# A new order for the opening of an adaptive-layernorm block, with separate buffers for two modulation rows

## Chip, cores and metric

The kernel runs on one core of a Trainium2 chip. The metric is the device time of one execution in microseconds, as the median of repeated runs.

## The reference, cut to what matters

The program computes one transformer-like block on x of shape (2, 4096, 512). A conditioning vector c gives six modulation rows per batch entry. The first half of the block normalizes x, applies two of the rows, computes three projections with a linear recurrence along the sequence, and adds the result to x through a third row. The second half does the same with a feed-forward part in blockwise FP4.

```python
mod = (_silu(L0_c) @ L0_wmod).reshape(L0_c.shape[0], 6, 1, -1)
sa, ca, ga, sb, cb, gb = (mod[:, 0], mod[:, 1], mod[:, 2], mod[:, 3], mod[:, 4], mod[:, 5])
ga = (2 * (ga >= 0) - 1) * jnp.maximum(jnp.abs(ga), 0.25)      # gb likewise
h = _layernorm(x, axis=-1) * (1 + ca) + sa
x = x + ga * attn(h, W_qkva, gamma)
h = _layernorm(x, axis=-1) * (1 + cb) + sb
x = x + gb * ffn(h, w_gate, w_up, w_down)
# attn: hn = h / |h| * sqrt(512) * gamma;  q, kv, a = split(hn @ W_qkva.T)
#       y_t = sigmoid(a_t) * y_{t-1} + kv_t;  result q * y
```

## The kernel before, in words

**Stages.** The program has two halves. The first (the loop over slots from line 751 on) does the recurrence: x is cut into 16 blocks of 512 rows, and each block into four output groups e of 128 channels, so that there are 64 slots. In a slot, `mix` (line 382) multiplies the transposed block `xT` with the transposed weights `wqT` of group e: three parts (2, 1, 0: gate, kv, q), each with 12 matmuls of 128x512, in fp16 high and low halves. In slot 0 alone, the matmuls are cut into four pieces of 128 columns, one for each row tile. The second half (from line 939 on) is the feed-forward part.

**What has to be ready before the first matmuls of slot 0.** `start()` (line 640) does it, in one order written out by hand. Inside `tc.manual_schedule` (line 747), the instructions of every engine run in the order in which the program issues them; SP, which issues the loads and the transposes, also runs in that order. `start()` mixes these chains:

- Modulation. `load_mod(s, pieces)` (208) loads the 512x512 weights of row s; `mod_spread` (216) multiplies them on TensorE with the conditioning vector `sc` spread over 128 columns, which gives the row on all partitions; ACT copies the two results to `ca[0]` and `sa[0]`. `mod_rows` (228) makes the same row for both batch entries in two partitions, and `mod_store` (255) copies that to `row` on ACT and writes it to DRAM by a DMA of POOL. `row` has one buffer. The PSUM tiles of these steps (`side`, 75) have two buffers.
- Weights of group e and part p. `load_part` (205), multiply by gamma (`gamma_qkva`, 278, on POOL or DVE), sum of squares on ACT (`square_qkva`, 281), inverse root (`inverse_qkva`, 285: one DVE step and a power on POOL), high half (`hi_qkva`, 301, on ACT or DVE), low half on DVE and the transpose on SP's DMA queue (`lo_qkva`, 310). `gain_qkva` (293) prepares the scale for the outputs.
- Rows of x, tile g of 128 rows. `norm_load` (328), `norm_moments` (336, DVE), `norm_stats` (339, DVE and POOL), `norm_center` (342, DVE), `norm_shift` (345, DVE), `norm_square` (348, ACT), `norm_gain` (355, DVE or POOL, then a power on POOL), `norm_hi` (362, ACT), `norm_lo` (368, DVE, then the transpose on SP's queue into `xT`).

**What start leaves to the slots.** Weights of groups 0 and 1 and the tiles 0 to 3 are finished in `start()`; tile 4 is carried up to its gain. Slot 0 issues, in this order: the matmuls of e=0, `mod_columns(2)` on TensorE, `norm_hi(4)`, the gammas (POOL) and squares (ACT) of group 2, `norm_moments(6)`, `norm_lo(4)`, and the steps of tile 5 up to its gain, then `scale_qkva(2)`. Slot 1 begins with e=1's matmuls and the halves and transposes of group 2, and goes on with tile 5 and the gammas of group 3; slot 2 has the transposes of group 3, slot 3 the last tile of block 1. `gates`, `scan`, `read_out` and `halves` treat the outputs of the slot before; `halves` (423) writes `yh`, one buffer, from slot 1 on.

Of the kernel before, what the change touches and what calls it, by code (L numbers as in the profile page):

```python
# [7 lines left out]
F32 = mybir.dt.float32  # L8
# [3 lines left out]
AF = mybir.ActivationFunctionType  # L12
# [5 lines left out]
P = 128  # L18
D = 512
KC = D // P  # L20
B = 2
# [22 lines left out]
def tile_adaln_block(  # L44
# [13 lines left out]
    V, A, G, T, S = nc.vector, nc.scalar, nc.gpsimd, nc.tensor, nc.sync  # L58
# [19 lines left out]
    mhalf = ctile([P, 4], F32, "mhalf")  # L78
# [103 lines left out]
    apool = pa.enter_context(tc.tile_pool(name="apool", bufs=1))  # L182

    def atile(shape, dtype, name, bufs=1):
        return apool.tile(shape, dtype, name=name, tag=name, bufs=bufs)
# [13 lines left out]
    with nc.allow_non_contiguous_dma(reason="c is 4 KB"):  # L199
        for b in range(B):  # L200
            S.dma_start(cT[:, :, b], c[b].rearrange("(k p) -> p k", p=P))
    A.activation(sc, cT, AF.Sigmoid)
    V.tensor_mul(sc, sc, cT)

    def load_part(e, part):
        S.dma_start(wq[e, part], w_qkva[part * D + e * P : part * D + (e + 1) * P, :])

    def load_mod(s, pieces=1):
        w = KC // pieces
        for k in range(0, KC, w):  # L210
            S.dma_start(
                wm[s][:, k : k + w, :],
                wmod[k * P : (k + w) * P, s * D : (s + 1) * D].rearrange("(k p) e -> p k e", p=P),
            )
# [13 lines left out]
    def mod_rows(s):  # L228
        pm = side((P, D))
        for k in range(KC):  # L230
            T.matmul(pm[:B, :], sc[:, k, :], wm[s][:, k, :], start=k == 0, stop=k == KC - 1)
        return s, pm[:B, :]
# [19 lines left out]
            out=dst, in0=dst, scalar=1.0, in1=mag, op0=ALU.subtract, op1=ALU.mult  # L252
        )

    def mod_store(s, pm):
        row = apool.tile([B, D], F32, name="row", tag="row", bufs=1)
        if s == 5:
            signed_floor(row, pm, apool.tile([B, D], F32, name="mag", tag="y", bufs=3))
        else:
            A.activation(row, pm, AF.Copy, bias=1.0 if s in (1, 4) else 0.0)  # L260
        G.dma_start(modd[s], row)
# [12 lines left out]
    def load_qkva(e):  # L274
        for part in (2, 1, 0):
            load_part(e, part)

    def gamma_qkva(e, part, engine=G):
        engine.tensor_tensor(wq[e, part], wq[e, part], gam, ALU.mult)

    def square_qkva(e, part):
        sq = work.tile([P, D], BF16, name="sq", tag="sq", bufs=1)
        A.activation(sq, wq[e, part], AF.Square, accum_out=us[:, e, part : part + 1])

    def inverse_qkva(e, a=0, b=3):
        V.tensor_scalar(rs[:, e, a:b], us[:, e, a:b], 1e-36, 2.0**-28, ALU.max, ALU.mult)
        G.tensor_tensor(rs[:, e, a:b], rs[:, e, a:b], mhalf[:, : b - a], ALU.pow)
# [5 lines left out]
    def gain_qkva(e):  # L293
        V.tensor_scalar(
            us[:, e, :], us[:, e, :], 1e-36, 2.0**-28 / (XGAIN * XGAIN), ALU.max, ALU.mult
        )
        G.tensor_tensor(us[:, e, :], us[:, e, :], phalf[:, :3], ALU.pow)
# [3 lines left out]
    def hi_qkva(e, part, on_act):  # L301
        w = wq[e, part]
        hl = whl[e, part] = new_hl()
        rsc = rs[:, e, part : part + 1]
        if on_act:
            A.activation(hl[:, 0, :], w, AF.Copy, scale=rsc)
        else:
            V.tensor_scalar(hl[:, 0, :], w, rsc, None, ALU.mult)

    def lo_qkva(e, part):  # L310
        w = wq[e, part]
        hl = whl.pop((e, part))
        r = part * KC + e
        V.scalar_tensor_tensor(
            out=hl[:, 1, :],
            in0=w,
            scalar=rs[:, e, part : part + 1],
            in1=hl[:, 0, :],
            op0=ALU.mult,
            op1=ALU.subtract,  # L320
        )
        S.dma_start_transpose(wqT[:, :, r * P : (r + 1) * P], flat(hl))
# [5 lines left out]
    def norm_load(g):  # L328
        i, t = divmod(g, KC)
        if i not in xrows:  # L330
            xrows[i] = apool.tile([P, KC, D], F32, name="xr", tag="xr", bufs=4)
        xld[g] = xrows[i][:, t, :]
        b, t0 = divmod(g * P, N)
        S.dma_start(xld[g], x[b, t0 : t0 + P, :])

    def norm_moments(g):
        xstat[g] = moments(xld[g])

    def norm_stats(g):
        xstat[g] = mean_rstd(xstat[g])  # L340

    def norm_center(g):
        xh[g] = center(xld.pop(g), xstat[g][0], ca[g * P // N])

    def norm_shift(g):
        shift(xh[g], xstat.pop(g)[1], sa[g * P // N])

    def norm_square(g):
        h = xh[g]
        sq = work.tile([P, D], BF16, name="sq", tag="sq", bufs=1)  # L350
        ss = small.tile([P, 1], F32, name="ss", tag="ss")
        A.activation(sq, h, AF.Square, accum_out=ss)
        xh[g] = h, ss

    def norm_gain(g, engine=V):
        h, ss = xh[g]
        engine.tensor_scalar(ss, ss, 1e-24, 1.0 / (D * XGAIN * XGAIN), ALU.max, ALU.mult)
        rn = small.tile([P, 1], F32, name="rn", tag="rn")
        G.tensor_tensor(rn, ss, mhalf[:, 0:1], ALU.pow)
        xh[g] = h, rn  # L360

    def norm_hi(g):
        h, rn = xh[g]
        hl = new_hl()
        A.activation(hl[:, 0, :], h, AF.Copy, scale=rn)
        xh[g] = h, rn, hl

    def norm_lo(g, xT):
        h, rn, hl = xh.pop(g)
        V.scalar_tensor_tensor(  # L370
            out=hl[:, 1, :], in0=h, scalar=rn, in1=hl[:, 0, :], op0=ALU.mult, op1=ALU.subtract
        )
        t = g % KC
        S.dma_start_transpose(xT[:, :, t * P : (t + 1) * P], flat(hl))
# [263 lines left out]
    sa = [ctile([P, D], F32, "sa0", tag="mod_s0"), None]  # L638

    def start():  # L640
        load_mod(1, 2)
        norm_load(0)
        load_mod(0, 2)
        load_part(0, 2)
        S.dma_start(gam, gamma.partition_broadcast(P))
        norm_load(1)
        load_part(0, 0)
        norm_load(2)
        load_part(0, 1)
        load_part(1, 2)  # L650
        load_part(1, 0)
        load_part(1, 1)
        norm_load(3)
        norm_load(KC)
        norm_load(KC + 1)
        pc = mod_spread(1, 0)
        ps = mod_spread(0, 0)
        r1 = mod_rows(1)
        r0 = mod_rows(0)
        norm_moments(0)  # L660
        norm_stats(0)
        A.activation(ca[0], pc, AF.Copy, bias=1.0)
        norm_center(0)
        gamma_qkva(0, 2, G)
        norm_moments(1)
        norm_stats(1)
        square_qkva(0, 2)
        gamma_qkva(0, 0, V)
        inverse_qkva(0, 2, 3)
        norm_moments(2)  # L670
        square_qkva(0, 0)
        gamma_qkva(0, 1, V)
        hi_qkva(0, 2, True)
        inverse_qkva(0, 0, 1)
        square_qkva(0, 1)
        lo_qkva(0, 2)
        hi_qkva(0, 0, True)
        inverse_qkva(0, 1, 2)
        norm_stats(2)
        norm_center(2)  # L680
        hi_qkva(0, 1, True)
        lo_qkva(0, 0)
        lo_qkva(0, 1)
        load_mod(2)
        gamma_qkva(1, 2, G)
        A.copy(sa[0], ps)
        norm_center(1)
        norm_shift(0)
        square_qkva(1, 2)
        norm_shift(1)  # L690
        norm_square(0)
        norm_square(1)
        norm_gain(0)
        norm_moments(3)
        norm_gain(1)
        norm_shift(2)
        norm_hi(0)
        norm_hi(1)
        norm_lo(0, xT)
        norm_square(2)  # L700
        norm_lo(1, xT)
        norm_gain(2)
        norm_stats(3)
        norm_center(3)
        norm_hi(2)
        norm_shift(3)
        norm_lo(2, xT)
        norm_square(3)
        norm_gain(3)
        gamma_qkva(1, 1, V)  # L710
        gamma_qkva(1, 0, V)
        norm_hi(3)
        inverse_qkva(1, 2, 3)
        square_qkva(1, 1)
        norm_lo(3, xT)
        square_qkva(1, 0)
        inverse_qkva(1, 1, 2)
        hi_qkva(1, 2, False)
        inverse_qkva(1, 0, 1)
        lo_qkva(1, 2)  # L720
        hi_qkva(1, 1, True)
        hi_qkva(1, 0, True)
        lo_qkva(1, 1)
        lo_qkva(1, 0)
        gain_qkva(0)
        load_qkva(2)
        norm_moments(KC)
        norm_stats(KC)
        norm_center(KC)
        norm_load(KC + 2)  # L730
        load_qkva(3)
        norm_shift(KC)
        norm_square(KC)
        norm_moments(KC + 1)
        norm_gain(KC)
        norm_stats(KC + 1)
        gain_qkva(1)
        mod_store(*r1)
        mod_store(*r0)

    units, coming = [], []
    gate = rows = None
# [278 lines left out]
```

## Time and profile before

| | us |
|---|---|
| median of 3 runs | 1957.3 (1956.27 to 1957.99) |
| the profiled execution | 1956.05 |
| its span, first to last instruction | 1954.2 |
| PE busy in the span | 1909.9 |
| DVE, ACT, POOL busy | 1607.7, 991.3, 423.8 |
| PE busy from 0 to 93 us | 62.7 of 93 |

PE is TensorE's matmul queue, DVE VectorE, ACT ScalarE, POOL GpSimd, SP the engine that issues most DMAs. Times in the lines are microseconds from the span's start. A line of the view in order of time gives start, length, engine, source line, instruction, output and inputs with their shapes, and in brackets how long the engine had been idle and what released it. A line that stands for several instructions (x36) is one stretch of the same kind. The mean granted TensorE clock of the execution is 0.992 of full speed.

### The profile page before, as it was taken

To read this page: it belongs to the slowest core of one execution; us is meant where nothing else is said; L and a number is where in the kernel's file an instruction comes from. 1 tells how busy PE (TensorE), PEld (TensorE's weight loads), DVE (VectorE), ACT (ScalarE), POOL (GpSimd) and SP (SyncE) were. 2 spreads that over 40 slices of the span, in tenths; PEclk is the share of its full clock that TensorE was granted. 3 is DMA by queue.
4 is the path that set the end of the run, shared out by engine and by line. 5 is a ranking of instruction groups with operands and counts; after the bars stand their busy time and mean duration, and the time that the engine had idled before them with its cause. 6 is when DMAs were issued, how large, how long until landed. Compare 5 with 4: busy or idle time off the path is not lost.

```text
span 1954.2 us, 25678 instructions
## 1 busy us (share of the span) xinstructions
PE 1909.9 (98%) x9220; PEld 902.4 (46%) x9220; DVE 1607.7 (82%) x2673; ACT 991.3 (51%) x1704; POOL 423.8 (22%) x603
## 2 busy tenths in 40 slices
PE   6699999999999999999999999999999999999998
PEld 4244444444444444444444444444444444444444
DVE  5777879999958988888888888888888888888865
ACT  3444467777755544544444454444445444444432
POOL 3554456666530100000000000001000000000000
PEclk8899999999999999999999999999999999999999
DMA  7597679999853343443343335334433433433333
GB/s 232 106 250 205 172 156 207 205 205 199 180 126 63 72 89 62 74 82 63 62 82 74 62 74 91 64 63 87 74 63 73 82 64 62 81 75 63 67 62 51
DMA packets 482943, 206.39 MB, mean 106 GB/s; under 512 B 439494, under 2 KB 440774, under 8 KB 482816
## 3 DMA queue, kind: packets, MB, share of 16 engines
q1 hardware_dynamic: 468080, 170.98, 40.9%
q0 software_dynamic: 14736, 33.78, 10.2%
q8 instruction: 72, 1.18, 0.3%
q14 instruction: 55, 0.45, 0.1%
HBM read 62.85 MB, written 33.58 MB: 49 GB/s over the span
## 4 chain that ended last, share of the span: by engine, by line
PE 79%; issue 5%; DVE 1%; DMA 1%; ACT 0%; POOL 0%; SPq 0%; POOLq 0%; ACTq 0%; DVEq 0%
PE mm L856 44%; PE sd L903 21%; PE mm L391 14%; DMA ld<-out_dram 0%; POOL out_dram L926 0%; DMA xT<-hl 0%; DVE ld L172 0%; DVE y L418 0%; DVE hl L370 0%; DVE ld L166 0%; DVE st L153 0%; DVE y L409 0%; ACT sq L583 0%; DVE xn L106 0%; SPq L265 0%
## 5 line engine op out<-in xcount | busy, mean ns | idle before, releaser
L856 PEld LDWEIGHTS <-x2T 128*128 128x128 f16 x4608 | 450.9, 98 | 469.4 <-issue 1.2
L391 PE MATMUL mm<-xT,wqT 128*128 128x512 f16 (+1 forms) x2412 | 510.2, 375 | 26.9 <-DMA wqT<-hl 13.1
L856 PE MATMUL mm<-wuT,x2T 128*128 128x512 f16 (+1 forms) x2304 | 487.7, 361 | 1.0 <-DVE hid L876 1.0
L856 PE MATMUL mm<-wgT,x2T 128*128 128x512 f16 (+1 forms) x2304 | 487.7, 361 | 0.0
L903 PE MATMUL sd<-wdT,hT 128*128 128x512 f16 x2112 | 465.8, 379 | 0.0
L391 PEld LDWEIGHTS <-wqT 128*128 128x128 f16 x2412 | 233.7, 100 | 305.0 <-issue 28.9
L903 PEld LDWEIGHTS <-hT 128*128 128x128 f16 x2112 | 206.7, 98 | 242.7
L871 ACT ACTIVATE silu<-mm,u 128x512 f32<-128x512 f32 (+1 forms) x192 | 124.7, 650 | 286.1 <-PE mm L856 282.4
L876 DVE SCALAR_TENSOR_TENSOR hid<-mm,u,silu 128x512 f32<-128x512 f32 (+1 forms) x192 | 128.6, 673 | 139.6 <-PE mm L856 130.6
L585 POOL TENSOR_SCALAR rstd<-vs 128x1 f32<-128x1 f32 x64 | 14.6, 228 | 985.9 <-ACT sq L583 985.9
L143 ACT ACTIVATE u<-ud,rms 128x1 f32<-128x1 f32 x64 | 18.9, 295 | 278.0 <-DVE rms L139 278.0
L120 ACT ACTIVATE sle<-sl 128x512 f16<-128x512 f32 (+2 forms) x162 | 146.9, 907 | 0.0
L113 ACT ACTIVATE she<-sh 128x1408 bf16<-128x1408 bf16 (+1 forms) x128 | 128.3, 1003 | 4.0
L926 POOL DMA_DIRECT2D out_dram<-o x65 | 58.0, 897 | 276.2 <-DVE o L923 272.3
L409 DVE TENSOR_TENSOR_SCAN y<-sig,cy,mm 128x512 f32<-128x512 f32 x56 | 71.7, 1280 | 49.3 <-ACT sig L403 22.1
L122 DVE SCALAR_TENSOR_TENSOR xn<-hid,xn 128x1408 f32<-128x1408 f32 x64 | 103.6, 1619 | 3.7 <-ACT hid L116 3.7
L106 DVE TENSOR_TENSOR xn<-hid,inv 128x1408 f32<-128x1408 f32 x64 | 104.0, 1625 | 2.2
L125 DVE SCALAR_TENSOR_TENSOR hhl<-hid,xn 128x1408 f16<-128x1408 f32 x64 | 104.0, 1625 | 2.2
L425 ACT COPY yh<-y 128x1024 uint16<-128x1024 uint16 x64 | 66.9, 1046 | 76.3 <-DVE y L418 72.4
L147 DVE TENSOR_REDUCE amh<-hid 128x88 f32<-128x1408 f32 x64 | 103.7, 1620 | 2.2
L116 ACT ACTIVATE hid<-xn 128x1408 f32<-128x1408 f32 x64 | 88.2, 1378 | 30.9 <-DVE xn L106 30.9
L441 POOL TENSOR_TENSOR xr<-xr,y 128x512 f32<-128x512 f32 x64 | 81.4, 1272 | 53.9 <-ACT y L433 52.5
(113 smaller groups left out, 1921.9 us busy)
## 6 DMA issues: line engine op xcount, KB each, us to landing
xr<-in_L_attn_x_dram SPq DMA_DIRECT2D x64, 256.0 KB, 3.2
out_dram<-xr POOLq DMA_DIRECT2D x64, 256.0 KB, 3.9
ld<-out_dram SPq DMA_DIRECT2D x64, 256.0 KB, 2.9
out_dram<-o POOLq DMA_DIRECT2D x63, 256.0 KB, 3.9
ld<-in_L_ffn_w_gate_dram SPq DMA_DIRECT2D x22, 256.0 KB, 3.1
ld<-in_L_ffn_w_up_dram SPq DMA_DIRECT2D x22, 256.0 KB, 3.4
scratch<-in_L_wmod_dram SPq DMA_DIRECT2D x4, 1024.0 KB, 5.4
ld<-in_L_ffn_w_down_dram SPq DMA_DIRECT2D x16, 256.0 KB, 3.1
```

The source lines that it names most:

```text
L106: V.tensor_tensor(blocks(xn), blocks(src), spread(inv, nb), ALU.mult)
L113: A.activation(blocks(she), spread(sh, nb), AF.Copy, scale=WPEAK)
L116: A.activation(a, xn, AF.Abs, scale=MAGIC)
L120: A.activation(blocks(sle), spread(sl, nb), AF.Copy, scale=WPEAK)
L122: V.scalar_tensor_tensor(out=xn, in0=a, scalar=FLOOR, in1=xn, op0=ALU.max, op1=ALU.add)
L125: V.scalar_tensor_tensor(out=nq, in0=a, scalar=FLOOR, in1=xn, op0=ALU.max, op1=ALU.subtract)
L147: V.tensor_reduce(am, src.rearrange("p (b k) -> p b k", k=QB), AX.X, ALU.max, apply_absolute_value=True)
L391: T.matmul(pp[:, t : t + width], wqT[:, wp * KC + k, r * P : (r + 1) * P], xT[:, xp * KC + k, t : t + width], start=n == 0, stop=n == 3 * ...
L856: T.matmul(pp[:, : n1 - n0], x2T[:, xp * KC + k, :], wt[:, wp * KC + k, n0:n1], start=n == 0, stop=n == 3 * KC - 1,)
L871: A.activation(sl[:, :w], pairs[j][0][:, :w], AF.Silu, scale=u[:, 0:1])
L876: V.scalar_tensor_tensor(out=hid[:, n0:n1], in0=pairs[j][1][:, : n1 - n0], scalar=u[:, 1:2], in1=sl[:, : n1 - n0], op0=ALU.mult, op1=ALU.mult,
L903: T.matmul(pd, hT[:, hp * IC + k, :], wdT[:, wd_chunk(wp, k), :], start=n == 0, stop=n == 3 * IC - 1,)
```

## The change

It touches three places.

1. Ahead of the sigmoid of c, ACT runs a sigmoid on four constants (`warm`).
2. `mod_store` takes the name of the buffer; row 1 of the opening goes to the buffer `yh`, row 0 to `row`. Both stores move from the end of `start()` to a place behind `norm_hi(3)`.
3. `start()` is written in a new order. The weights of modulation row 1 come in four pieces; gamma and the three weight parts of group 0 are loaded ahead of the x tiles 1 to 3; the weights of group 2 are loaded ahead of the transposes of group 1; the x tiles 4 and 5 later than before, and modulation row 2 earlier. All gammas of groups 0 and 1 run on DVE (two of them ran on POOL). The first step of `norm_gain` runs on POOL for tiles 0 to 4 (on DVE before). The steps of tile 0 and the weights of group 0 are interleaved differently.

```diff
     with nc.allow_non_contiguous_dma(reason="c is 4 KB"):
         for b in range(B):
             S.dma_start(cT[:, :, b], c[b].rearrange("(k p) -> p k", p=P))
+    warm = atile([P, 4], F32, "warm")
+    A.activation(warm, mhalf, AF.Sigmoid)
     A.activation(sc, cT, AF.Sigmoid)
     V.tensor_mul(sc, sc, cT)
 
@@
-    def mod_store(s, pm):
-        row = apool.tile([B, D], F32, name="row", tag="row", bufs=1)
+    def mod_store(s, pm, tag="row"):
+        row = apool.tile([B, D], F32, name="row", tag=tag, bufs=1)
         if s == 5:
             signed_floor(row, pm, apool.tile([B, D], F32, name="mag", tag="y", bufs=3))
         else:
@@
     sa = [ctile([P, D], F32, "sa0", tag="mod_s0"), None]
 
     def start():
-        load_mod(1, 2)
+        load_mod(1, KC)
         norm_load(0)
         load_mod(0, 2)
-        load_part(0, 2)
         S.dma_start(gam, gamma.partition_broadcast(P))
-        norm_load(1)
-        load_part(0, 0)
-        norm_load(2)
-        load_part(0, 1)
-        load_part(1, 2)
-        load_part(1, 0)
-        load_part(1, 1)
-        norm_load(3)
-        norm_load(KC)
-        norm_load(KC + 1)
+        for part in PARTS:
+            load_part(0, part)
+        for g in range(1, KC):
+            norm_load(g)
+        for part in PARTS:
+            load_part(1, part)
+        load_mod(2)
         pc = mod_spread(1, 0)
         ps = mod_spread(0, 0)
         r1 = mod_rows(1)
         r0 = mod_rows(0)
+
         norm_moments(0)
         norm_stats(0)
         A.activation(ca[0], pc, AF.Copy, bias=1.0)
+        a, b_, c_ = PARTS
+        gamma_qkva(0, a, V)
+        square_qkva(0, a)
+        gamma_qkva(0, b_, V)
+        square_qkva(0, b_)
+        inverse_qkva(0, a, a + 1)
+        gamma_qkva(0, c_, V)
+        inverse_qkva(0, b_, b_ + 1)
         norm_center(0)
-        gamma_qkva(0, 2, G)
+        hi_qkva(0, a, True)
+        square_qkva(0, c_)
         norm_moments(1)
+        hi_qkva(0, b_, True)
+        inverse_qkva(0, c_, c_ + 1)
+        lo_qkva(0, a)
         norm_stats(1)
-        square_qkva(0, 2)
-        gamma_qkva(0, 0, V)
-        inverse_qkva(0, 2, 3)
+        A.copy(sa[0], ps)
+        lo_qkva(0, b_)
+        hi_qkva(0, c_, True)
+        norm_shift(0)
+        norm_square(0)
+        norm_center(1)
+        lo_qkva(0, c_)
+        norm_gain(0, G)
+        norm_shift(1)
+        norm_hi(0)
+        norm_square(1)
         norm_moments(2)
-        square_qkva(0, 0)
-        gamma_qkva(0, 1, V)
-        hi_qkva(0, 2, True)
-        inverse_qkva(0, 0, 1)
-        square_qkva(0, 1)
-        lo_qkva(0, 2)
-        hi_qkva(0, 0, True)
-        inverse_qkva(0, 1, 2)
         norm_stats(2)
+        norm_lo(0, xT)
+        norm_gain(1, G)
+        norm_hi(1)
         norm_center(2)
-        hi_qkva(0, 1, True)
-        lo_qkva(0, 0)
-        lo_qkva(0, 1)
-        load_mod(2)
-        gamma_qkva(1, 2, G)
-        A.copy(sa[0], ps)
-        norm_center(1)
-        norm_shift(0)
-        square_qkva(1, 2)
-        norm_shift(1)
-        norm_square(0)
-        norm_square(1)
-        norm_gain(0)
         norm_moments(3)
-        norm_gain(1)
+        norm_lo(1, xT)
+        norm_load(KC)
         norm_shift(2)
-        norm_hi(0)
-        norm_hi(1)
-        norm_lo(0, xT)
         norm_square(2)
-        norm_lo(1, xT)
-        norm_gain(2)
         norm_stats(3)
         norm_center(3)
+        norm_gain(2, G)
         norm_hi(2)
         norm_shift(3)
+        norm_square(3)
         norm_lo(2, xT)
-        norm_square(3)
-        norm_gain(3)
-        gamma_qkva(1, 1, V)
-        gamma_qkva(1, 0, V)
+        norm_gain(3, G)
+        gamma_qkva(1, a, V)
         norm_hi(3)
-        inverse_qkva(1, 2, 3)
-        square_qkva(1, 1)
+        mod_store(*r1, tag="yh")
+        mod_store(*r0)
+        square_qkva(1, a)
+        gamma_qkva(1, b_, V)
         norm_lo(3, xT)
-        square_qkva(1, 0)
-        inverse_qkva(1, 1, 2)
-        hi_qkva(1, 2, False)
-        inverse_qkva(1, 0, 1)
-        lo_qkva(1, 2)
-        hi_qkva(1, 1, True)
-        hi_qkva(1, 0, True)
-        lo_qkva(1, 1)
-        lo_qkva(1, 0)
-        gain_qkva(0)
+        norm_load(KC + 1)
         load_qkva(2)
+        inverse_qkva(1, a, a + 1)
+        gamma_qkva(1, c_, V)
+        square_qkva(1, b_)
+        square_qkva(1, c_)
         norm_moments(KC)
+        hi_qkva(1, a, False)
+        inverse_qkva(1, b_, b_ + 1)
         norm_stats(KC)
+        lo_qkva(1, a)
+        inverse_qkva(1, c_, c_ + 1)
+        hi_qkva(1, b_, True)
+        hi_qkva(1, c_, True)
         norm_center(KC)
+        lo_qkva(1, b_)
+        norm_shift(KC)
+        norm_square(KC)
+        lo_qkva(1, c_)
         norm_load(KC + 2)
         load_qkva(3)
-        norm_shift(KC)
-        norm_square(KC)
+        norm_gain(KC, G)
+        gain_qkva(0)
         norm_moments(KC + 1)
-        norm_gain(KC)
         norm_stats(KC + 1)
         gain_qkva(1)
-        mod_store(*r1)
-        mod_store(*r0)
```

## The prediction

> **What bounds the kernel now.** I read the page's first two parts, then TensorE's (PE's) waits, then PE's line of time up to 100 us, then the queues of ACT, DVE, POOL and SP between 36 and 66 us.
>
> ```profile
> PE 1909.9 (98%) x9220; PEld 902.4 (46%) x9220; DVE 1607.7 (82%) x2673; ACT 991.3 (51%) x1704; POOL 423.8 (22%) x603
> ...
> PE   6699999999999999999999999999999999999998
> ```
>
> PE is busy 98% of the span; only its first two slices (0 to 98 us) show real holes (the last, at 8, holds the end). An edit of the opening is worth what those holes shrink, if PE is the bound afterwards.
>
> ```profile
> 5.85 9.02 PE L219 MATMUL sd<-scratch,sc 128*128 128x512 f32 x16 [5.85 <-DMA scratch<-in_L_wmod_dram]
> 14.80 3.60 PE L231 MATMUL sd<-scratch,sc 128*2 128x512 f32 x8
> 20.41 3.59 PE L231 MATMUL sd<-scratch,sc 128*2 128x512 f32 x8 [2.01 <-ACT sa L686]
> 29.06 10.36 PE L391 MATMUL mm<-xT,wqT 128*128 128x128 f16 x144 [5.05 <-DMA xT<-hl]
> 41.33 4.72 PE L238 MATMUL sd<-sc,scratch 128*128 128x2 f32 x32 [1.91 <-ACT row L260]
> 45.90 10.27 PE L391 MATMUL mm<-xT,wqT 128*128 128x512 f16 x36
> 64.10 9.72 PE L391 MATMUL mm<-xT,wqT 128*128 128x512 f16 x36 [7.93 <-DMA wqT<-hl]
> 79.05 10.77 PE L391 MATMUL mm<-xT,wqT 128*128 128x512 f16 x36 [5.22 <-DMA wqT<-hl]
> 92.14 8.14 PE L391 MATMUL mm<-xT,wqT 128*128 128x512 f16 x37 [2.32 <-DMA xT<-hl]
> ```
>
> PE's line of time: start, length, what, and in brackets the idle time ahead. The reader sees seven holes; the last ends at 92.14, and after it PE runs on (20.00 of 20 us busy from 100 to 120). So the end of the program moves as much as that 92.14 moves. The holes at 64.10 and 79.05 wait for transposed weights, not for anything PE did late. Their cause is in the other queues:
>
> ```profile
> 40.70 0.57 ACT L260 ACTIVATE row<-sd 2x512 f32<-2x512 f32 x1
> 50.05 0.59 ACT L260 ACTIVATE row<-sd 2x512 f32<-2x512 f32 x1 [8.78 <-DMA modd<-row]
> 50.55 0.70 ACT L365 ACTIVATE hl<-ld,rn 128x512 f16<-128x512 f32 x1
> ...
> 50.95 0.54 POOL L261 DMA_DIRECT2D modd<-row  x1 [6.93 <-ACT row L260]
> 51.51 3.73 POOL L279 TENSOR_TENSOR scratch<-scratch,gam 128x512 f32<-128x512 f32 x3
> ...
> 45.77 0.69 DVE L153 BATCH_NORM_STATS2 st<-xr 128x6 f32<-128x512 f32 x1 [4.64 <-DMA xr<-in_L_attn_x_dram]
> 51.28 4.51 DVE L370 SCALAR_TENSOR_TENSOR hl<-ld,rn,hl 128x512 f16<-128x512 f32 x1 [4.82 <-ACT hl L365]
> 60.04 0.48 DVE L308 TENSOR_SCALAR hl<-scratch,rs 128x512 f16<-128x512 f32 x1 [2.38 <-POOL rs L287]
> ```
>
> ACT stands 8.78 us because the second row (r0) needs the one `row` buffer that the first row's DMA (issued 43.23, 6.7 us to landing) still reads. Behind it stand ACT's norm_hi(4), then DVE's norm_lo(4), and on POOL the r0 DMA and the three gamma_qkva(2). From there one chain runs on: norm_lo(4) ends 55.79, center and shift of tile 5 end 57.37, ACT's square 58.2, POOL's gain 59.17 and rs(2) 60.0, DVE's hi(2) at 60.04, the first transpose lands and PE starts at 64.10. Slots 2 and 3 hang on the same DVE/ACT/POOL round (60.04 to 74.97 to the tile-7 transpose at 87.82), so 92.14 hangs on it too.
>
> **What the Trainium skill says.** (1) SBUF — State Buffer, "SBUF: two separate sides": DVE and GpSimd share a port pair under an exclusive lock; the loser of a DVE op with two SBUF inputs against a GpSimd op blocks fully. The trace agrees: norm_lo(4) took 4.51 us instead of 0.75, ending 0.5 us after POOL's 3.73 us of gamma. (2) TensorE: Matmul & The Clock Gate, "What's actually happening": the array falls to half clock after an idle window of some 3.4 us. It agrees: weight loads are 0.43 us apart after 45.90, and 36 matmuls take 9.72 to 10.77 us in the opening against 8.14 for 37 at 92.14. (3) ScalarE: Activation LUTs, "What ACT_TABLE_LOAD costs": about 1283 ns for the load; here 1.28 us at 3.57.
>
> **The change, part by part.** I walk the new queues in program order, with durations and spacings of the trace of before. Spacings used: DVE two-input op 0.67 us (0.75 to its result), bn_stats 0.60, ACT op 0.62 (0.73 to its sum or result), 0.04 to 0.1 between engines, POOL pow 0.55 alone and 0.93 beside DVE, POOL gain 0.9 in all, rstd 1.0 to 1.2, a transpose 2.8 to landing and 1.35 apart.
>
> *Warm sigmoid, four pieces of modulation weights.* The table load leaves the wait for cT (3.57): sc is done near 3.8, not 5.08. A 256 KB piece is half of the one that landed at 5.70, at 0.65 us per 256 KB (x1 13.70, W 14.27, x2 14.96, W 15.6): about 5.0. PE starts 0.85 earlier. It costs one tiny ACT op and two more DMA issues of 0.5 us on SP, hidden, since eight transfers are then in flight and bandwidth sets the landings. On the path it is worth 0: ca is copied by 11.5, and center(0) is not reached before 15.4.
>
> *Loads.* In the new order gam lands at 10.74+1.73=12.5 (13.02 before), the three weight parts of e=0 at 13.1, 13.75, 14.4, x1 to x3 at 15.05 to 16.35, e=1 by 18.3, the 1 MB of modulation rows 2 by 21. They delay the first wqT transposes somewhat; PE needs those only at 25.6.
>
> *DVE takes all gammas of e=0 and 1* (two more, 0.68 each = 1.4), gives five gains to POOL (5x0.15) and meets no POOL gamma before slot 0 (center(1) took 1.75 instead of 0.75: 1.0 back). Net about -0.4 us, so the gain is order. The walk, for weights: DVE gamma a 13.15 to 13.83; ACT square a to 14.65; DVE inverse, POOL pow to 15.45; ACT hi a at 15.5; meanwhile DVE gamma b, c and center(0) to 16.2; square c to 16.85, pow c to 17.7; lo a 16.95, lo b 17.7. ACT's sa copy falls at 17.4 (19.79 before), so r0 on PE starts at 18.0 (20.41). For tiles: shift(0) 18.4, square to 19.93, POOL gain to 20.9 or 21.4, hi 21.2 to 21.9, norm_lo(0) 21.95 to 22.7, transpose 22.75, landed 25.6 (29.06 before). Tile 1: rstd(2) stands ahead of its gain on POOL (to 24.1), norm_lo(1) 24.9. Tile 2: shift 25.6, square to 27.13, rstd(3) to 27.7, gain to 28.6, norm_lo(2) 29.4. Tile 3: square behind norm_hi(2) to 30.0, gain to 30.95, norm_lo(3) 31.75 (32.66 before), landed near 35.6 (36.9). So POOL's longer chain for the gains costs the early lead: 3.4 us at tile 0 are 1.3 at tile 3. mix(0, e=0) ends about 38 (39.42); mod_columns follows at once, since its bank was freed by the r1 copy at 32; e=1 runs 42.7 to 52.5 if it starts cold as before.
>
> *Row buffers.* r1 goes to the yh buffer, r0 to row, both copied at 31.6 to 32.8: two ACT ops of 0.58 in start, POOL DMAs of 0.78 and 0.54 ending near 33.6. POOL's pow(1,a), which DVE's hi(1,a) waits for, stands behind them; square(1,a) ends 33.5, so that is 0.1 us. yh is next written by halves in slot 1, long after. The 8.78 us wait is gone.
>
> *Rest of start.* hi(1,a) on DVE 34.85, lo(1,a) 35.5, center(4) 36.2, lo(1,b) 36.9, shift(4) 37.6, lo(1,c) 38.5, its transpose off SP by 40.6, then x6's load: landed about 43.5 (45.77 before; three weight loads now go ahead of the e=1 transposes). DVE's last gain 40.1 (40.99 before). POOL ends gain(1) at 42.9 and runs the gammas of e=2 from 42.95 to 46.7 (51.51 to 55.24 before).
>
> *Slot 0.* What is late next, once ACT is free, is POOL's gammas: norm_lo(4), ready at 44.1 after bn_stats of x6, is blocked by them. Two ends for this unknown: it slips between two gammas and ends at 45.5 to 46, or it is held to the end as before (46.7+0.5=47.2). I take the second. Then aggregate, center and shift to 48.7, square 49.5, gain 50.4, rs(2) 51.35, DVE hi(2) at 51.4 against 60.04: 8.6 us sooner. The first end gives 50.0, or 10.0 sooner. In the other direction, six POOL steps on the path at 0.93 instead of 0.55 give 2.3 less: 6.3 sooner. I take 8.3, a little for such slowing.
>
> *Afterwards.* e=2 starts at 51.7+4.1=55.8; PE was ready at 52.5, so that hole is 3 us, not 7.9. e=3 comes 14.95 later as before, the last tile of block 1 13.1 after that: 83.8 instead of 92.14. PE's floor does not bind (52.5+2x9.7=72). Whether PE is cold there is worth up to 1.7 (3.4 us at half rate) either way at 92.14, where it was warm.
>
> The sum: profiled time 1956.05 (span 1954.2 plus 1.85 around it) - 8.3 = 1947.75; the median of the runs shown is 1957.3, 1.25 above the profiled one, so 1949.0.
>
> **The rivals.** *A, the walk is too tight:* DVE carries 1.4 us more gammas and ten POOL hand-offs lie in its way; if start ends 3 us later than walked, the gain is about 5: 1952.3. For it: ACT and POOL waits of 0.2 to 1.2 us in the trace; against it: its DVE end, 40.1, is only 0.9 below that of before. *B, more:* norm_lo(4) is not held, and a warm PE: 10 to 12 gained, 1946. *C, no change:* x6's transfer takes the place of the row wait. It stands behind the transposes on SP; if it landed 7 us after issue, at 47.6 or later with the POOL gammas held up by the last gain, some 2 to 5 us are left: 1954 or a little more. Against it: 4.5 us with a full queue before, and fewer transfers ahead now. *D, slower:* POOL's two row DMAs now stand in the middle of start. If POOL was held until each landed (6.7 us as the first one took), 13.4 us would fall on pow(1,a), DVE's hi(1,a) and all behind: 13.4-8.3=5 later, 1962.3; it decides from 12.2 us of hold on. Against it: in the trace POOL went from the DMA at 50.95 to gamma at 51.51, before that row had landed (1.6 us).
>
> **How the numbers follow.** Forecast 0.70 (1946.7 to 1951), A 0.13, B 0.06, C 0.07, D 0.04. About 0.2%, or 3.9 us, is what a measurement can tell: faster means below 1953.4, which forecast, B and most of A give: 0.88; same 0.08; slower 0.04. The range 1945.5 to 1953.0 leaves out part of A and B, C and D.
>
> **What would show it.** Right: no ACT wait on the row DMA; first PE matmul at 5.0, xT of tile 0 at 25.6; wqT waits of about 3 and 5 us; steady PE from about 84. Wrong: an ACT or DVE wait of over 3 us in 33 to 50 us, the e=2 hole as long as before, or steady PE later than 88.

## The result and the profile after

The changed kernel takes 1952.2 us (median of 16 runs, 1948.56 to 1955.23), the kernel before 1956.78 us (16 runs, 1953.9 to 1959.77). The ratio is 0.9976, with a 95% interval of 0.9968 to 0.9983: 4.7 us less, between 3.3 and 6.3. The forecast was 8.3 us less. One run of e11_e10_e5 below (3565.95 us) and one of the kernel before taken beside it (6295.61 us) were in a slow state and are left out of every median and ratio. The profiled execution took 1952.46 us with a span of 1950.6, against 1956.05 and 1954.2.

TensorE's line of time of the changed kernel, with the same columns as in the prediction (lines of the changed file are two higher, L393 is `mix`):

```profile
5.13 9.20 PE L221 MATMUL sd<-scratch,sc 128*128 128x512 f32 x16 [5.13 <-DMA scratch<-in_L_wmod_dram]
...
19.09 3.60 PE L233 MATMUL sd<-scratch,sc 128*2 128x512 f32 x8 [1.24 <-ACT sa L678]
26.94 6.93 PE L393 MATMUL mm<-xT,wqT 128*128 128x128 f16 x72 [4.25 <-DMA xT<-hl]
34.92 2.17 PE L393 MATMUL mm<-xT,wqT 128*128 128x128 f16 x36 [1.05 <-DMA xT<-hl]
38.41 2.17 PE L393 MATMUL mm<-xT,wqT 128*128 128x128 f16 x36 [1.32 <-DMA xT<-hl]
40.41 4.59 PE L240 MATMUL sd<-sc,scratch 128*128 128x2 f32 x32
44.86 10.36 PE L393 MATMUL mm<-xT,wqT 128*128 128x512 f16 x36
58.51 2.76 PE L393 MATMUL mm<-xT,wqT 128*128 128x512 f16 x12 [3.29 <-DMA wqT<-hl]
62.17 5.34 PE L393 MATMUL mm<-xT,wqT 128*128 128x512 f16 x24 [0.89 <-DVE y L411]
73.44 9.74 PE L393 MATMUL mm<-xT,wqT 128*128 128x512 f16 x36 [5.93 <-DMA wqT<-hl]
```

The hole before the modulation columns (1.91 us before) is gone, and the one before group 2 (58.51) is 3.29 instead of 7.93, with 0.89 more inside group 2. The hole before group 3 (73.44) has stayed (5.93, before 5.22). The lines of the other queues that answer to those shown of before:

```profile
34.41 1.05 ACT L262 ACTIVATE row<-sd 2x512 f32<-2x512 f32 x2
35.29 1.30 POOL L263 DMA_DIRECT2D modd<-row  x2 [1.54 <-ACT row L262]
45.95 3.71 POOL L281 TENSOR_TENSOR scratch<-scratch,gam 128x512 f32<-128x512 f32 x3
48.77 0.69 DVE L153 BATCH_NORM_STATS2 st<-xr 128x6 f32<-128x512 f32 x1 [5.30 <-DMA xr<-in_L_attn_x_dram]
49.38 0.83 DVE L372 SCALAR_TENSOR_TENSOR hl<-ld,rn,hl 128x512 f16<-128x512 f32 x1
54.44 0.49 DVE L310 TENSOR_SCALAR hl<-scratch,rs 128x512 f16<-128x512 f32 x1 [2.36 <-POOL rs L289]
```

ACT copies both rows back to back; the 8.78 us wait does not occur. DVE's wait for x tile 6 has stayed, at 5.30 us instead of 4.64, and is now the longest there. DVE's first `hi` of group 2 comes at 54.44 instead of 60.04.

Block 1's first matmuls begin a stretch without further holes up to about 250 us. They are in these two lines, the first before, the second after:

```profile
92.14 39.01 PE L391 MATMUL mm<-xT,wqT 128*128 128x512 f16 x180 [2.32 <-DMA xT<-hl]
```

```profile
86.83 40.70 PE L393 MATMUL mm<-xT,wqT 128*128 128x512 f16 x180 [3.66 <-ACT cy L414]
```

Block 1 starts 5.31 us earlier, but its first 180 matmuls take 1.69 us longer. So the modulation rows behind them start at 127.46 instead of 131.08, 3.62 us earlier. That is the whole difference of the two spans (3.6).

### The profile page after: what moved, and what is told of

The parts are those of the page before. It is cut to its first block, busy times and chain, and to the rows that moved or that the text cites. A ratio compares the mean times of both kernels' runs of the same rounds, so it can differ in the third digit from the quotient of the medians.

```text
span 1950.6 us, 25677 instructions
## 1 busy us (share of the span) xinstructions
PE 1909.8 (98%) x9220; PEld 902.5 (46%) x9220; DVE 1603.2 (82%) x2670; ACT 993.5 (51%) x1705; POOL 423.3 (22%) x606
## 4 chain that ended last, share of the span: by engine, by line
PE 79%; issue 5%; DVE 1%; DMA 0%; POOL 0%; SPq 0%; ACT 0%; POOLq 0%; ACTq 0%; DVEq 0%
PE mm L857 44%; PE sd L904 21%; PE mm L393 14%; DMA xT<-hl 0%; POOL out_dram L927 0%; DVE ld L172 0%; DVE hl L372 0%; DVE ld L166 0%; DVE y L420 0%; DVE xn L106 0%; SPq L575 0%; DVE st L153 0%; SPq L267 0%; SPq L529 0%; DVE hl L129 0%
## 5 line engine op out<-in xcount | busy, mean ns | idle before, releaser
L393 PE MATMUL mm<-xT,wqT 128*128 128x512 f16 (+1 forms) x2412 | 510.2, 375 | 26.7 <-DMA xT<-hl 11.6
L393 PEld LDWEIGHTS <-wqT 128*128 128x128 f16 x2412 | 234.1, 100 | 304.5 <-issue 29.4
```

What stands on the lines that cost most here:

```text
L393: T.matmul(pp[:, t : t + width], wqT[:, wp * KC + k, r * P : (r + 1) * P], xT[:, xp * KC + k, t : t + width], start=n == 0, stop=n == 3 * ...
```

## The experiments

The theory: the wait for the one row buffer was the delay, and what came next is a mixture of POOL's and DVE's small steps, the load of tile 6 and POOL's gammas. The first rival: the new order of loads and steps carries the gain. All kernels are edits of the changed kernel unless said otherwise. The ratio of each experiment is to runs of the kernel before taken beside it, whose medians lie between 1956.2 and 1957.0; the medians in the table are as measured, so two of them can differ by some 0.8 us for that alone. Besides the median, each is read at three places of its profile: DVE's first gamma (POOL's in the two kernels with the old order), DVE's first `hi` of group 2, and the start of block 1.

| kernel | first gamma | hi of group 2 | block 1 | its first 180 matmuls | median us | ratio to before, 95% interval |
|---|---|---|---|---|---|---|
| before | 13.09 | 60.04 | 92.14 | 39.01 | 1956.78 | |
| changed | 13.94 | 54.44 | 86.83 | 40.70 | 1952.2 | 0.9976 (0.9968 to 0.9983) |
| e1_rows_only | 13.28 | 54.15 | 86.23 | 40.70 | 1950.83 | 0.9965 (0.9951 to 0.9979) |
| e2_order_only | 13.50 | 56.64 | 89.01 | 40.70 | 1954.9 | 0.9989 (0.9982 to 0.9995) |
| e3_x6_early | 14.15 | 54.09 | 86.95 | 41.1 | 1951.79 | 0.9972 (0.9961 to 0.9983) |
| e4_busy_pe | 14.38 | 54.87 | 87.60 | 39.01 | 1950.99 | 0.9971 (0.9959 to 0.9982) |
| e5_x6_gamma_dve | 13.56 | 50.35 | 81.55 | 39.01 | 1950.32 | 0.9969 (0.9958 to 0.9981) |
| e6_e5_busy | 13.93 | 50.94 | 82.14 | 39.01 | 1949.31 | 0.9963 (0.9951 to 0.9976) |
| e7_old_first | 12.63 | 52.81 | 84.92 | 40.69 | 1948.69 | 0.9963 (0.9950 to 0.9977) |
| e8_gain_dve | 13.64 | 52.17 | 84.61 | 39.01 | 1949.38 | 0.9964 (0.9951 to 0.9976) |
| e9_two_pieces | 12.74 | 53.23 | 85.35 | 39.01 | 1950.49 | 0.9970 (0.9958 to 0.9981) |
| e10_first_gain | 12.57 | 51.39 | 83.52 | 39.01 | 1947.69 | 0.9960 (0.9946 to 0.9974) |
| e11_e10_e5 | 13.01 | 48.41 | 79.31 | 39.01 | 1943.4 | 0.9936 (0.9922 to 0.9950) |

The intervals reach some 1.3 to 2.7 us to either side, so steps of 1 or 2 us are read from the traces. Each kernel has one profile. Between kernels whose openings up to `norm_center(0)` do the same, the first gamma differs by up to 0.9 us (13.50 to 14.38), so a difference of block 1 below about 1 us is no finding either.

### e1_rows_only: the kernel before, with two buffers

```diff
-    def mod_store(s, pm):
-        row = apool.tile([B, D], F32, name="row", tag="row", bufs=1)
+    def mod_store(s, pm, tag="row"):
+        row = apool.tile([B, D], F32, name="row", tag=tag, bufs=1)
...
-        mod_store(*r1)
+        mod_store(*r1, tag="yh")
```

> The kernel before with one edit: modulation row 1 of the opening gets the yh buffer, and the order, the loads and the engines stay as they were. Theory (the row wait was the delay, and what came next in the changed kernel was the load of x tile 6): ACT's 8.8 us wait is gone; x6 still lands at about 45.8, POOL's gammas of group 2 run from about 44.6 to 48.3 and hold norm_lo(4) to about 48.8 (55.79 before), so group 2's matmuls start near 57.1, group 3's near 72.1, block 1 near 85.2 (92.14 before; 86.83 in the changed kernel). Time 5.3 to 7 us below before, as much as the whole change or more. Rival (the new order carries the gain): norm_lo(4) stays behind something else in the old order, block 1 starts at 90 or later, and the time is within 2 us of before.

The profile of this kernel, the ACT, POOL and DVE queues:

```profile
41.97 1.05 ACT L260 ACTIVATE row<-sd 2x512 f32<-2x512 f32 x2
...
45.83 4.24 POOL L279 TENSOR_TENSOR scratch<-scratch,gam 128x512 f32<-128x512 f32 x3
46.83 0.69 DVE L153 BATCH_NORM_STATS2 st<-xr 128x6 f32<-128x512 f32 x1 [4.45 <-DMA xr<-in_L_attn_x_dram]
...
47.45 1.52 DVE L370 SCALAR_TENSOR_TENSOR hl<-ld,rn,hl 128x512 f16<-128x512 f32 x1
```

The wait is gone, and block 1 starts at 86.23, 5.9 us before that of the kernel before. The theory's 85.2 is missed by 1 us. This execution's opening ran 1.2 us late (center(0) at 13.34 instead of 12.11), and so did POOL's gammas (45.83, reckoned 44.6). norm_lo(4) was not held to their end: it took 1.52 us and finished at 48.97, while the third gamma ran to 50.07. But DVE's next two-input operation, tile 5's center, then took 1.65 us instead of 0.71. The rival falls: this edit of three lines does as much as the whole change, at block 1 and in the median; the intervals overlap, and 0.6 us at block 1 is no finding, so that it does more is not shown.

### e2_order_only: the changed kernel with one buffer

```diff
-        mod_store(*r1, tag="yh")
+        mod_store(*r1)
```

> The changed kernel with both modulation rows in the one row buffer again; all else as changed. Theory: ACT's copy of row 0 waits for the DMA of row 1, which took 2.1 us from its issue at 35.3, so ACT and all behind it stand some 2.5 us in the middle of start, and POOL's second row DMA comes that much later; block 1 starts near 89.3 instead of 86.8 and the time is about 2.5 us above the changed kernel. Rival (moving the stores to an earlier place is enough, the buffer is not needed): block 1 near 86.8 and the time of the changed kernel within 1 us.

```profile
37.06 0.59 ACT L262 ACTIVATE row<-sd 2x512 f32<-2x512 f32 x1 [2.53 <-DMA modd<-row]
```

The wait is back, at 2.53 us instead of 8.78, and the first row's DMA took 2.1 us from issue to landing, against 6.7. In the kernel before eight loads had been issued in the 3.7 us ahead of it, here none for 7 us; in e1_rows_only, where the loads stand ahead of it again, it took 5.7. Block 1 starts at 89.01, 2.2 us later than with two buffers, as the theory said (89.3). With the stores moved but not split, about 2 of the 4.7 us remain (0.9989). The two parts overlap: block 1 comes 5.9 us earlier by the buffers alone (e1_rows_only), 3.1 by all the rest alone, and 5.3 by both.

### e3_x6_early: the load that DVE waits for

```diff
         norm_load(KC + 1)
+        norm_load(KC + 2)
         load_qkva(2)
...
-        norm_load(KC + 2)
         load_qkva(3)
```

> The changed kernel with the load of x tile 6 moved on SP's queue from behind the transposes of group 1 to ahead of the loads of group 2. Theory (that load, which landed 4.9 us after its issue at 43.84, is what set norm_lo(4)): moments of tile 6 no longer wait 5.3 us, norm_lo(4) runs at about 44.2 before POOL's gammas begin at 46, and what is late next is ACT's square behind POOL's third gamma (49.7): DVE's hi of group 2 comes near 53.0 instead of 54.4, block 1 near 85.4 instead of 86.8; time 1 to 1.5 us below the changed kernel. Rival (POOL's slow small steps in start set it, the load only lands beside them): no move of block 1 beyond 0.3 us.

```profile
44.33 0.75 DVE L372 SCALAR_TENSOR_TENSOR hl<-ld,rn,hl 128x512 f16<-128x512 f32 x1
...
47.03 3.71 POOL L281 TENSOR_TENSOR scratch<-scratch,gam 128x512 f32<-128x512 f32 x3
...
54.09 0.48 DVE L310 TENSOR_SCALAR hl<-scratch,rs 128x512 f16<-128x512 f32 x1 [2.18 <-DMA xr<-in_L_attn_x_dram]
```

norm_lo(4) runs 5 us earlier, and hi of group 2 moves by 0.35 us. The theory's size was wrong here: the 5.30 us wait for tile 6 lies beside POOL's gammas. These now begin 1.1 us later, because POOL's rstd and power steps run beside DVE's center and shift; ACT's third square and the square of tile 5 follow the gammas. The longest wait of DVE here was worth almost nothing by itself.

### e4_busy_pe: the clock before block 1

```diff
+            if slot == KC:
+                idle = side((P, TB))
+                for n in range(15):
+                    T.matmul(idle, wqT[:, 0, :P], wqT[:, 1, :TB], start=n == 0, stop=n == 14)
             cur = mix(i, xT, e) if slot < NS else None
```

> The changed kernel with 15 matmuls of 128x512 more, whose result nobody reads, ahead of block 1's first matmuls: TensorE runs them in the hole between group 3 and block 1. Theory (that hole lets the clock fall, which costs 1.7 us after it): block 1 still starts near 86.8, but at 0.216 us a matmul from the start, so that the first 100 take 21.6 us instead of 23.4, and the time is 1.5 to 1.9 us below the changed kernel. Rival (the slow first matmuls wait for something else): 23.4 us for the first 100 as now, and the time unchanged or up to 1 us longer.

```profile
84.37 3.40 PE L765 MATMUL sd<-wqT 128*128 128x512 f16 x15
87.60 39.01 PE L393 MATMUL mm<-xT,wqT 128*128 128x512 f16 x180
```

The granted TensorE clock of the changed kernel at this place (each line: the window, its length, PE busy, and behind the brackets the clock as a share of full speed, then the DMA share and GB/s):

```profile
86.00:90.00 4.00, 3.17 (x9) 0.67 0.72 168
90.00:94.00 4.00, 4.00 (x18) 0.90 1.21 179
```

In finer windows it is 1.00 until about 87.3 and 0.50 from there to about 90.8. In e4_busy_pe it is 1.00 throughout, and the 180 matmuls take 39.01 us, 1.69 less. So the slow first matmuls are the clock, and the rival falls. That the hole let the clock fall is not shown by this run: five kernels without added matmuls had holes of 2.45 to 3.48 us ahead of block 1 and ran at 39.01 as well (see the last section). Block 1 started 0.8 us later in this execution, 0.4 by a later group 3 and the rest by the added matmuls, which run up to its start. The median is 1.2 us below the changed kernel's; the intervals overlap, so a gain in time is not shown; the cost of the slow stretch in the changed kernel's trace is.

### e5_x6_gamma_dve and e6_e5_busy: POOL's gammas

```diff
                 for part in PARTS:
-                    gamma_qkva(slot + 2, part)
+                    gamma_qkva(slot + 2, part, V)
```

This is on top of the edit of e3_x6_early; e6_e5_busy has the added matmuls of e4_busy_pe as well.

> The changed kernel with the load of x tile 6 early, as in the run with that edit alone, and with the gammas of groups 2 and 3 in slots 0 and 1 on DVE instead of POOL. That earlier run moved DVE's hi of group 2 only from 54.44 to 54.09, because POOL's gammas then began at 47.0 and ended at 50.7, and ACT's last square and the square of tile 5 stood behind them. Theory (with the row wait and the load gone, POOL's gammas are the wait that is left): hi of group 2 near 51, no hole before group 2 or one under 1 us, group 3 near 69 (73.1), block 1 near 82.5 to 83.5 (86.8 changed); time 3 to 4.5 us below the changed kernel, 1947.7 to 1949.2 beside 1952.2. Rival (the slots' own round of DVE, ACT and POOL sets the pace, and DVE loses what POOL gains): block 1 at 86 or later.

> The kernel with x tile 6 early and the gammas of groups 2 and 3 on DVE, and in addition 15 matmuls, read by nobody, in the hole ahead of block 1. Theory (the cold clock is a term of its own): the first 180 matmuls of block 1 in 39.0 us instead of 40.7 and 1.7 us less in all, about 1946 to 1947.5, the fastest of all kernels here. Rival: block 1 starts later by what the added matmuls overrun, and the two offset each other.

With both edits hi of group 2 comes at 50.35, the hole before group 2 is gone, and block 1 starts at 81.55, 5.3 us before the changed kernel. The load should be worth something here: norm_lo(4) ran at 45.40, and it stands behind tile 6's moments, which the changed kernel could not start before 48.77. The gammas on DVE without the early load were not run. The medians are lower than the changed kernel's by 1.9 and 2.9 us, less than foretold. The lines from block 7 on, first in the changed kernel, then in e5_x6_gamma_dve:

```profile
291.60 248.80 PE L393 MATMUL mm<-xT,wqT 128*128 128x512 f16 x1152 [1.40 <-ACT sig L405]
```

```profile
285.15 250.49 PE L393 MATMUL mm<-xT,wqT 128*128 128x512 f16 x1152 [4.10 <-ACT sig L405]
```

The hole before block 7 grew from 1.40 to 4.10 us (4.22 in e6_e5_busy), and the matmuls behind it and block 15's (32.93 us instead of 31.24) each had a slow stretch of 1.69 us that the changed kernel had not there. So a lead of 6.5 us at block 7 ended as 3.5 in the spans. For e6_e5_busy, the added matmuls brought nothing, since block 1 was at full rate in e5_x6_gamma_dve already.

### e7_old_first and e9_two_pieces: the first loads

```diff
-    warm = atile([P, 4], F32, "warm")
-    A.activation(warm, mhalf, AF.Sigmoid)
...
-        load_mod(1, KC)
+        load_mod(1, 2)
```

e7_old_first has both parts of this, e9_two_pieces the second alone.

> The changed kernel without the warm sigmoid, and with the first modulation weights in two loads again as before. Theory (the earlier first matmul is hidden behind the weights' gammas and the DVE queue): TensorE starts near 5.85 instead of 5.13, and nothing from norm_center(0) on moves by more than 0.5 us; block 1 within 0.5 us of 86.8, the time within 1 us of the changed kernel. Since x tile 0 and the first weights landed 0.8 to 1.2 us later in the changed kernel than reckoned, a move of block 1 to the earlier side by up to 0.8 is possible. Rival (carrying the first tile and weights to TensorE is where the gain lies): block 1 later by 0.7 us or more.

> The changed kernel with the first modulation weights in two loads instead of four, and the warm sigmoid kept. Theory (the two more load issues on SP, some 0.5 us each, put every later load of the opening back, as the run without both parts suggests: first gamma at 12.63 there against 13.94): first gamma near 12.6 to 12.7, block 1 near 85 (86.83), time within 1 us of the run without both parts (1948.7). Rival (the warm sigmoid is what costs): first gamma near 13.9, block 1 near 86.8.

The first DVE gamma of the changed kernel, and then of e7_old_first:

```profile
13.94 1.33 DVE L281 TENSOR_TENSOR scratch<-scratch,gam 128x512 f32<-128x512 f32 x2 [3.74 <-DMA scratch<-in_L_attn_W_qkva_dram]
```

```profile
12.63 1.32 DVE L279 TENSOR_TENSOR scratch<-scratch,gam 128x512 f32<-128x512 f32 x2 [3.81 <-DMA scratch<-in_L_attn_W_qkva_dram]
```

TensorE starts at 5.66 instead of 5.13 in e7_old_first, and all else comes earlier: the first gamma by 1.3 us, block 1 by 1.9. So the four pieces do carry the first weights to TensorE 0.5 us sooner, and put everything behind them on SP's queue 1.3 us later (gam landed at 13.2 against 11.9). e9_two_pieces has the early gamma (12.74) with the warm sigmoid kept: the pieces cost, the sigmoid does not. The four kernels with two pieces in this order have the first gamma at 12.57 to 13.01 (mean 12.74), the seven with four pieces at 13.50 to 14.38 (mean 13.87), so the cost is clear of the spread, at some 1.1 us. The forecast's 0 for this part had the wrong sign.

### e8_gain_dve: the small steps on POOL

```diff
-        norm_gain(3, G)
+        norm_gain(3)
```

and the same for tiles 0, 1, 2 and 4.

> The changed kernel with the first step of norm_gain of tiles 0 to 4 on DVE again instead of POOL. Theory (POOL's small steps beside DVE's two-input operations, 0.58 to 0.80 us instead of 0.25, are where the walk of start was too short): norm_lo of tiles 2 and 3 come 0.5 to 1.5 us earlier than 31.36 and 34.54, start ends 1 to 2 us earlier, the load of x tile 6 is issued earlier than 43.84, and block 1 starts 1 to 2 us before 86.8; time 1 to 2 us below the changed kernel. Rival (DVE's own queue is what is long): no move, or 0.7 us later for five more DVE steps.

POOL's steps for tile 3, first in the changed kernel, then in this one:

```profile
32.03 0.78 POOL L359 TENSOR_SCALAR ss<-ss 128x1 f32<-128x1 f32 x1 [1.46 <-ACT sq L354]
32.89 0.86 POOL L361 TENSOR_TENSOR rn<-ss,mhalf 128x1 f32<-128x1 f32 x1
```

```profile
31.03 0.93 POOL L361 TENSOR_TENSOR rn<-ss,mhalf 128x1 f32<-128x1 f32 x1 [1.69 <-DVE ss L359]
```

The step on POOL, of one element a partition, takes 0.78 us there beside DVE's two-input operations (0.24 to 0.80 over the five tiles); on DVE it took 0.15. norm_lo(2) and norm_lo(3) come at 30.13 and 32.74 instead of 31.36 and 34.54, and block 1 at 84.61 instead of 86.83. The theory holds. The time is 2.8 us below the changed kernel's, more than foretold; in the trace 1.69 us more come from block 1, which ran at full clock here.

### e10_first_gain and e11_e10_e5: the terms together

e10_first_gain joins e7_old_first and e8_gain_dve; e11_e10_e5 adds the edits of e5_x6_gamma_dve.

> The changed kernel with two terms undone together: first loads in two pieces without the warm sigmoid, and the first step of norm_gain on DVE. Theory (they lie one behind the other on the same path of start, so that they add): block 1 near 86.8 - 1.9 - 2.2 = 82.7, and the time 1.5 to 3 us below each of the two alone, 1946 to 1948. Rival (either removes the same wait): block 1 near 84.5, time as with either alone, 1948.7 to 1949.4.

> The kernel with both terms undone, and in addition x tile 6 early and the gammas of groups 2 and 3 on DVE. Theory (the row wait gone, the opening is no longer held by loads or POOL): block 1 near 78 to 79.5. At the end less is left: in the run with x tile 6 early and these gammas on DVE, block 1 was 5.3 us earlier than in the changed kernel but the span only 3.5 us shorter, with a new hole of 4.1 us at 285 us behind ACT's sigmoid, so the stage from 190 to 300 us, where DVE carries the weights' maxima too, gives part back. Time 1945.5 to 1948.5, no more than 1.5 us below the kernel with both terms undone. Rival (no give-back): 3 us or more below it.

e10_first_gain starts block 1 at 83.52, between the full sum (82.7) and the rival (84.5). e11_e10_e5 starts it at 79.31, 4.2 us earlier, and takes 1943.4 us, 4.3 below e10_first_gain. That the two agree so well is chance: the profiled executions differ by 2.6 (spans 1943.2 and 1945.8), because block 15 had a slow stretch in this one (32.93 us) and not in e10_first_gain's (31.24). My expectation of a give-back fell here: the hole before block 7 was 1.21 us. It beats both kernels (0.9936, 0.9922 to 0.9950). What made that hole 4.10 us in e5_x6_gamma_dve stays open. TensorE in its opening:

```profile
43.84 17.31 PE L391 MATMUL mm<-xT,wqT 128*128 128x512 f16 x72 [0.96 <-DMA wqT<-hl]
66.34 10.17 PE L391 MATMUL mm<-xT,wqT 128*128 128x512 f16 x36 [5.19 <-DMA wqT<-hl]
79.31 39.01 PE L391 MATMUL mm<-xT,wqT 128*128 128x512 f16 x180 [2.79 <-DMA xT<-hl]
```

Groups 1 and 2 are one stretch now, and the hole before group 3 is the largest left.

## Why the prediction was right, and where its sizes were off

**The number.** The forecast was 1949.0 us, 8.3 less; 1952.2 was measured, which is rival A's 1952.3. A's reason, a start that ends 3 us late, is what the runs show; that the four pieces cost part of it no rival had named. The stated range held because it took in part of A, not because the sum was near. Rival C's sign came as well: tile 6 landed at 48.77, later than its 47.6. But e3_x6_early removed that wait and gained 0.35 us at `hi` and nothing at block 1, so C's reason alone is not the lag. D fell: POOL's next step began at 36.60, right behind the two row DMAs.

**The signs.** No ACT wait on the row came; TensorE started at 5.13 (foretold 5.0), tile 0's matmuls at 26.94 (25.6), steady TensorE at 86.83 (84). One sign of being wrong came too: waits of over 3 us between 33 and 50 us, 5.30 on DVE for tile 6 and 3.14 on ACT for POOL's gamma. It was no good sign, since a wait can lie beside another one.

**The row wait.** Right, and shown by removing it alone: e1_rows_only moved block 1 by 5.9 us with the old order. "Slots 2 and 3 hang on the same round" held to within 0.3 us: from the end of norm_lo(4) to group 2 it took 8.3 us before and after, from group 2 to group 3 14.95 and 14.93, and on to block 1 13.1 and 13.4.

**The walk of start.** This term was mis-sized, as rival A put it (start ends 3 us late: a gain of about 5). DVE's last gain ran at 43.34, not 40.1; POOL's gammas began at 45.95, not 42.95; hi of group 2 came at 54.44, not 51.4. Two parts of the lag are shown. The loads: the first gamma ran at 13.94, not 13.15, because the walk let the four pieces cost nothing on SP's queue; taking them back gave 1.3 us there. The gains on POOL: I took 0.9 us in all where tile 3's two steps took from 32.03 to 33.75; taking them back gave 2.2 us at block 1. Together they gave 3.3 us there (e10_first_gain against the changed kernel), as much as was missing: there POOL's gammas began at 42.84 and hi of group 2 came at 51.39, against 42.95 and 51.4 in the walk.

**Tile 6.** Landed 48.77, not 43.5: the load took 4.9 us, not the 2.9 that I took for a queue with fewer transfers ahead. But e3_x6_early shows that this by itself cost 0.35 us at `hi`, which is within the spread.

**norm_lo(4) held by POOL.** I took the worse end, held through the third gamma. In the changed kernel the question hardly arose: behind tile 6's moments it began at 49.38, 0.28 us before the gammas ended, and took 0.83 us. The walk's end for it, 0.5 us after the gammas, came out (50.21 against 49.66), but by the load as much as by POOL. In e1_rows_only it took 1.52 us and ended 1.1 us before the gammas did, so there it slipped between two of them. What decides between this and the 4.51 us of before stays open.

**The clock.** Named as a range of 1.7 us, and taken as 0. It was 1.69 us against the changed kernel in its profile, behind a hole of 3.66 us instead of 2.32. My reading that the trace of before agrees with an idle window of 3.4 us was too quick: its half clock at 45.90 followed no hole longer than 1.91 us since 29.06. The forecast's 8.3 minus 3.0 for the walk is the 5.3 of block 1; minus 1.7 for the clock is the 3.6 of the spans. The medians differ by 4.6.

**"So the gain is order."** That clause of mine, on DVE's work, found no more than this: of the 5.3 us at block 1 the new order as a whole brought nothing beyond the buffers. What its better interleaving won, the pieces and the POOL gains took: undone together they put block 1 at 83.52, against 86.23 with the buffers alone (up to 1.2 us of it that run's late opening).

## What to carry to other kernels

A one-buffer tile that leaves through a DMA stalled the engine that wrote it next (8.78 us before, 2.53 in e2_order_only), and all that was queued behind it; a second buffer for it did here what a rewritten opening did. When such a stall goes, cost the chain behind it with the durations that the small steps have beside their neighbours (0.78 us, not 0.25), and count added load issues as a delay of the later loads on their queue (two of them: some 1.1 us here). A long wait is worth only what it sticks out beyond the wait beside it: 5.30 us of waiting for a load were worth 0.35 while POOL's gammas ran beside it.

## What the runs showed that I had not expected

A hole of little more than 2 us can be followed by a slow stretch of TensorE, and need not be. In the seven stretches of this kind whose clock was read in windows of 0.25 us, it was still full when the matmuls began again, fell to half 0.1 to 1.2 us later, and stayed there for 3.4 us; each cost 1.69 us (144 matmuls in 32.93 us or 31.24, the 180 of block 1 in 40.70 or 39.01). Ahead of blocks 1, 6 and 15 in all kernels here, holes of 3.66 us and more were all followed by one, and holes of 1.82 or less by none. In between, the length does not decide: there was a slow stretch behind 2.19 us (e4_busy_pe, 256.25) and 3.32 us (e1_rows_only, block 1), and none behind 2.67 us (changed, 543.07) and 3.48 us (e9_two_pieces, block 1). Ahead of block 6 all eleven holes of 2.19 to 2.59 us were followed by one, ahead of block 15 six of thirteen holes of 2.18 to 3.15. Why stays open.

With three or four such holes in a program, steps of 1.69 us come and go from run to run. The 16 runs of before cover 5.9 us, about 3.5 such steps. The mean clock on record fits: of the runs of the kernel before beside the experiments, the 18 with a mean clock of 0.991 took 1957.9 us on average, the 27 with 0.992 took 1956.0, and half clock for 3.4 of 1954 us lowers the mean by 0.0009. That this is the whole spread was not tried.
